# Group statistics by small DMA transfers instead of matrix products, a third output buffer, and a moved normalization, in a two-layer attention kernel

## The chip, the core and the metric

The kernel runs on one core of one Trainium2 chip. The metric is the device time of one execution in microseconds (us). The engines are called PE (TensorE, matrix products; PEld is its loading of weights), DVE (VectorE), ACT (ScalarE), POOL (GpSimd) and SP (SyncE, which only issues transfers). Each runs its own instructions in order and waits for others by semaphores. POOL and SP each have a queue of DMA transfers, in the order of their instructions.

## The reference

The input `x` is 4 images x 256 channels x 64 x 64, all in float32. Two layers are added to it, one after the other. Each first normalizes `x` over 32 groups of 8 channels, and it is this normalization that the change is about:

```python
def _gn(v, G=32, eps=1e-5):
    g = v.reshape(B_, G, C_ // G, H_, W_)
    m = jnp.mean(g, axis=(2, 3, 4), keepdims=True)
    s = jnp.var(g, axis=(2, 3, 4), keepdims=True)
    return ((g - m) / jnp.sqrt(s + eps)).reshape(v.shape)

x = x + _L0_conv_ref(_gn(x), ...)   # layer A below
x = x + _L1_conv_ref(_gn(x), ...)   # layer B below
```

Layer A is attention with 8 heads of 32 channels. Its queries are a 1x1 product of all 4096 points (`Wq`), its keys and values are 2x2 convolutions with stride 2 (1024 points), and a position term is added to the keys. Layer B takes q, k and v from one 1x1 product (`w_qkv`), attends within four areas of 1024 points, adds a 7x7 convolution of each channel's values, and ends in a 1x1 product (`w_proj`).

## The kernel before

**Units, steps, phases.** The attention of both layers is cut into 128 units: 8 blocks (layer A of images 0 to 3, then layer B of images 0 to 3) of 16 units, each unit being four heads and 512 queries. A unit has 8 steps, each of 128 keys. The main loop runs over 683 phases of one and a half steps. A phase issues, in this order: the scores of its own steps (PE, L428); the exponentials of them (ACT, L469 and L480); a slot of other work on PE; and the weighted sums of the phase before (PE, L494). DVE adds the exponentials up for the divisors (L504). The scores use three pairs of PSUM banks in turn, so the scores of a phase wait until ACT has emptied the pair that they write.

**The slot between.** In it stands one of four things: nothing; the divisors of a finished unit (`den`, L513); a function out of the list `quick`; or one, two or four "side parts". Side parts are the projections and convolutions, each cut with `yield` into two or four parts: q, k and v of layer A (`q0ps`, `k0ps`, `v0ps`), q and k of layer B (`q1ps`, `k1ps`), the values of layer B (`vals_ps`), the convolution (`conv_ps`, L1048) and the last product (`ops`). All but the convolution are issued by the helper at L167. How many parts a phase takes is set by the due times (`pressure`) and by `supply`, which spreads what is there and what will come over the next 24 phases at 13 slots in 16.

**The program is laid out by hand.** `at(g, j, f)` has `f` called at step `j` of unit `g`, and whatever `f` issues then goes to the ends of the engines' queues. What lies before unit 0 is issued ahead of the loop. `later(...)` puts normalizations (ACT, L392) into a list that is worked off when ACT has room, from a given phase on.

**Statistics.** `plan_norm` makes the scales of one normalization, called its key: A or B and the image. DVE aggregates the statistics of each channel (`aggregate`, L346); `means` multiplies them with `gmat`, a matrix of blocks of 1/8, so that each channel gets its group's mean (PE, L351), which ACT copies out of PSUM (L352); DVE adds each channel's squared deviation to its variance (L353 to L355); `variances` multiplies that with `gmat` again (PE, L359), ACT adds epsilon (L360), and POOL makes the reciprocal root and the shift (L363 to L368). In the loop, `means` and `variances` go through `soon` into `quick`, and a phase takes one of them if no task is begun, no unit ends in it, and the last was over two phases ago. A phase that takes one does no side part. Keys A of image 0 and A of image 1 are planned ahead of the loop, the other six inside it. The first reading of the scales is allowed four phases after they are `known`.

**Divisors.** For each finished unit, POOL issues `few` (L527), `recs` (L535) and four `rb` (L537) with DVE's reciprocals between them (L533), and DVE divides by `rb` (L540). The reciprocals are planned at step 0 of the second unit after, the division at step 7 of it.

**Values of layer B.** `values(t)` clears the edges of an output `vout` (DVE, L963 and L964), makes the product, copies it out (ACT, L975), and stores it twice (SP, L980 and L988: `vala` and `vals`). There are two buffers for `vout`. `load_v` loads a quarter of an area's values back from `vala` into one of four buffers `vc` (SP, L742), and `make_v` transposes it (DVE, L749). SP also loads the convolution's rows and matrices (`rows`, `share`, `band`, L1029 and L1032), in the same queue.

**q of layer A.** `fetch` loads a chunk `hq` (L108), and `norm_chunk` normalizes it from five phases after the load on.

Of the kernel before, what the change touches and what calls it, by code (L numbers as in the profile page):

```python
# [9 lines left out]
FP = mybir.dt.float32  # L10
# [5 lines left out]
P = 128  # L16
# [44 lines left out]
def direct_path(  # L61
# [129 lines left out]

    side, quick, quick_at = deque(), deque(), [-9]
    now, last = [-1], len(BLOCKS) * UNITS * NKT
# [20 lines left out]
    def supply():  # L214

        far = 24
        comes = [0] * (far + 1)
# [13 lines left out]
        for h in range(far):  # L231
            total += comes[h]
            least = min(least, total / max(1, (h + 1) * 13 / 16))
        return least
# [80 lines left out]

    def soon(f):

        if now[0] < 0:
            f()
        else:  # L320
            quick.append(f)

    stats, norms = {}, {}
# [11 lines left out]
    def plan_norm(key, g, j):  # L335

        name = f"{key[0]}{key[1]}"
        made = {}

        def aggregate():  # L340
            for tag, cols in (("mv", 2), ("gmean", 1), ("dev", 1), ("gvar", 1)):
                shape = [P, CT, cols] if cols > 1 else [P, CT]
                made[tag] = pool.tile(shape, FP, tag=tag, name=f"{tag}_{name}", bufs=2)
            mv = made["mv"]
            for t in range(CT):
                V.bn_aggr(out=mv[:, t, :], in_=stats[key][:, t].rearrange("p c s -> p (c s)"))  # L346
# [10 lines left out]
        def variances():  # L357
            ps = ps_side(f"gv_{name}")[:, :CT]
            T.matmul(ps, lhsT=gmat, rhs=made["dev"], start=True, stop=True)  # L359
            S.activation(made["gvar"], ps, AF.Identity, bias=eps)  # L360
            norm = pool.tile([P, 2, CT], FP, tag="norm", name=f"norm_{name}", bufs=8)
            shift, rstd = norm[:, 0, :], norm[:, 1, :]
            G.tensor_tensor(rstd, made["gvar"], neghalf, ALU.pow)  # L363
            if key == ("A", 0):
                V.scalar_tensor_tensor(shift, made["gmean"], -1.0, rstd, ALU.mult, ALU.mult)
            else:
                G.tensor_tensor(shift, made["gmean"], rstd, ALU.mult)
                G.tensor_scalar(shift, shift, -1.0, None, ALU.mult)  # L368
            norms[key] = shift, rstd
            known[key] = phase[0] if now[0] >= 0 else -4  # L370

        def quietly(f, n):
            f()
            if key == ("A", 0):
                keep_busy(n)

        if key == ("A", 0):
            at(g - 1, 0, lambda: keep_busy(44))
        at(g, j, aggregate)
        at(g, j + (2 if g >= 0 else 1), lambda: soon(lambda: quietly(means, 4)))  # L380
        at(g, j + (6 if g >= 0 else 3), lambda: soon(lambda: quietly(variances, 10)))

    def normalize(key, dst, src, t, by_vector=False):
        while key not in norms:
            while begun():
                advance()
            quick.popleft()()
        shift, rstd = norms[key]
# [162 lines left out]
    def plan_a(b, u, prep):  # L551
# [72 lines left out]
        for c in range(NCH):  # L624
            at(early + c // 2, 4 * (c % 2), lambda c=c: look(c))
            for t in range(CT):
                lag = (5 + 2 * t if b == 1 else 8 + 2 * t if b else 3)
                at(early + c // 2, 4 * (c % 2) + lag, lambda c=c, t=t: add_stats(c, t))
        plan_norm(key, early + (5 if b > 1 else 4), 3 if b > 1 else 4 if b else 1)
        for a in range(NAREA):  # L630
# [50 lines left out]
        for c in range(NCH):  # L681
            g = u + 2 * c
            at(g - 3, 4, lambda c=c: fetch(c))
            for t in range(CT):
                at(g - 2, 1 + 2 * t, lambda c=c, t=t: later(
                    ("hq", b, c), lambda: norm_chunk(c, t), after(key, fetched["q", c] + 5), True
                ))
# [17 lines left out]
    def plan_b(b, u):  # L705
# [34 lines left out]
        def load_v(a, n):  # L740
            vcs[a, n] = pool.tile([P, 2, 4 * TX, XT], FP, tag="vc", name=f"vc_{b}_{a}_{n}", bufs=4)
            nc.sync.dma_start(vcs[a, n], vala[b][a][:, :, 2 * n : 2 * n + 2].rearrange("t c h f x -> (t c) h f x"))  # L742
# [30 lines left out]
        for a in range(NAREA):  # L773
# [8 lines left out]
            for n in range(4):  # L782
                at(g - 4, 3 + 2 * n, lambda a=a, n=n: load_v(a, n))
                at(g - 2, 1 + 2 * n, lambda a=a, n=n: make_v(a, n))
        for c in range(NCH):
# [162 lines left out]
    def plan_values(b, c, start):  # L948
# [11 lines left out]
        def values(t):  # L960
            vout = pool.tile([P, RC, TX, XT], FP, tag="vout", name=f"vout_{b}_{c}_{t}", bufs=2)
            written.append(phase[0])
# [195 lines left out]
    before, credit = [], 0.0  # L1158
    while f < PHASES or before or plan or side or quick or norms_left or to_add or to_divide:
        now[0], phase[0] = step, f  # L1160
# [26 lines left out]
        elif due and not begun():  # L1187
# [6 lines left out]
            else:  # L1194
                rb = pool.tile([P, CH], FP, tag="p", name="rb", bufs=PB)
                V.reciprocal(rb, dens[g])
                spare.extend((dens.pop(g), rb))
        elif quick and not begun() and not cut and f < PHASES and f > quick_at[0] + 2:
            quick.popleft()()
            quick_at[0] = f  # L1200
        else:
# [14 lines left out]
        if f >= PHASES:  # L1216
            side_parts(2)
        if quick and f >= PHASES:
            quick.popleft()()
        while step < -(-3 * (f + 1) // 2):  # L1220
# [614 lines left out]
```

## Time and profile before

| | |
|---|---|
| median of 3 runs | 3063.1 us (3060.73 to 3066.85) |
| the profiled execution | 3063.53 us, its span 3061.5 us |
| mean granted clock of PE | 0.998 |
| exponential, 128x1024 (ACT, L469) | 1025 ns, x1194 |
| addition, 128x1024 (DVE, L504) | 1220 ns, x1790 |
| product with `gmat` (PE, L351 and L359) | 16 instructions each, 258 to 267 ns |
| `few`, `recs`, `rb` from issue to landing (POOL's queue) | 4.3, 3.8, 3.6 us in the median |
| HBM traffic over the span | 135 GB/s |

The page of the profile gives busy time by engine and, in 40 equal slices, the busy share in tenths, the granted clock of PE and the load of the 16 DMA engines. The timeline gives merged rows of one engine: start, duration, engine, line, what is written from what, how often, and in brackets the idle time before it and what ended that. Since products overlap in the array and their ends are modelled, the time that a block really took is the distance from its start to the next block's start. A list of waits has rows of "engine tile line <- what ended the wait: us in total, times, longest".

### The profile page before, as it was taken

How to read it: one execution, taken by the hardware profiler on the slowest of the kernel's cores; microseconds unless marked ns; L12 is line 12 of the kernel's file. 1: busy time of each engine (PE TensorE's matmuls, PEld its weight loads, DVE VectorE, ACT ScalarE, POOL GpSimd, SP SyncE). 2: the span in 40 equal slices, each digit the busy share in tenths (PEclk: the TensorE clock that was granted, in tenths of full speed). 3: DMA queues.
4: the chain of work that ended last, by engine and by line, in shares of the span. 5: the costliest groups of instructions: out<-in, count | busy, mean ns of one | idle time of the engine just before them, and what ended most of it. 6: DMA issues, size and time to landing. Idle time of an engine off the chain costs nothing.

```text
span 3061.5 us, 108320 instructions
## 1 busy us (share of the span) xinstructions
PE 3032.8 (99%) x47254; PEld 1280.0 (42%) x47254; DVE 2526.2 (83%) x2769; ACT 2455.9 (80%) x2988; POOL 433.8 (14%) x794
## 2 busy tenths in 40 slices
PE   9999999999999999999999999999999999999998
PEld 6444434444344444333444444444434444443332
DVE  3788988889887787878888888788878888888888
ACT  3888888888887888888888877788777787878885
POOL 0011111111111111111111111111111111111111
PEclk9999999999999999999999999999999999999999
DMA  5244533466354557777866677667755565553232
GB/s 191 51 101 98 126 92 73 109 142 165 83 140 133 143 152 175 189 161 194 204 175 162 156 176 185 152 171 178 176 127 145 144 159 143 149 139 79 50 71 62
DMA packets 644250, 422.73 MB, mean 138 GB/s; under 512 B 409740, under 2 KB 552572, under 8 KB 643768
## 3 DMA queue, kind: packets, MB, share of 16 engines
q1 hardware_dynamic: 619384, 380.11, 49.3%
q0 software_dynamic: 24384, 35.62, 5.1%
q8 instruction: 373, 6.11, 0.9%
q14 instruction: 109, 0.89, 0.1%
HBM read 317.28 MB, written 97.05 MB: 135 GB/s over the span
## 4 chain that ended last, share of the span: by engine, by line
PE 91%; DMA 3%; DVE 2%; ACT 2%; issue 2%; SPq 1%; POOL 0%; DVEq 0%; ACTq 0%; POOLq 0%
PE s L428 31%; PE av L494 26%; PE k0ps L167 4%; PE den L513 4%; PE v0ps L167 4%; PE q1ps L167 4%; PE k1ps L167 4%; PE conv_ps L1048 4%; PE q0ps L167 4%; PE ops L167 4%; PE vals_ps L167 3%; DVE acc L504 1%; ACT p L469 1%; DMA vals<-vout 1%; DMA rows<-vals 1%
## 5 line engine op out<-in xcount | busy, mean ns | idle before, releaser
L504 DVE TENSOR_TENSOR acc<-acc,p 128x1024 f32<-128x1024 f32 x1790 | 2117.4, 1220 | 382.7 <-PE av L494 285.7
L469 ACT ACTIVATE p<-s 128x1024 f32<-128x1024 f32 x1194 | 1159.8, 1025 | 419.3 <-PE s L428 407.6
L480 ACT ACTIVATE p<-s 128x1024 f32<-128x1024 f32 x598 | 619.8, 1036 | 1.5 <-DVE acc L504 0.7
L428 PE MATMUL s<-q,k_A 32*64 32x256 f32 (+1 forms) x10928 | 541.1, 494 | 4.1 <-ACT p L469 3.5
L428 PE MATMUL s<-q,k_B 32*64 32x512 f32 (+1 forms) x10912 | 537.1, 494 | 2.8 <-ACT p L469 2.4
L494 PE MATMUL av<-p,v_A 128*32 128x256 f32 (+1 forms) x4784 | 451.4, 486 | 0.0
L494 PE MATMUL av<-p,v_B 128*32 128x512 f32 (+1 forms) x4776 | 449.4, 487 | 0.0
L428 PEld LDWEIGHTS s<-q,k_B 32*64 32x64 f32 x10912 | 266.0, 130 | 325.1 <-PE s L428 60.4
L428 PEld LDWEIGHTS s<-q,k_A 32*64 32x64 f32 x10928 | 263.2, 130 | 329.1 <-PE s L428 58.5
L537 POOL DMA_DIRECT2D rb<-recs x508 | 251.4, 501 | 510.3 <-DMA recs<-few 497.9
L535 POOL DMA_DIRECT2D recs<-few x127 | 71.3, 561 | 1719.9 <-DVE sums L534 1600.3
L494 PEld LDWEIGHTS av<-p,v_B 128*32 128x32 f32 x4776 | 149.2, 110 | 264.5 <-issue 238.3
L494 PEld LDWEIGHTS av<-p,v_A 128*32 128x32 f32 x4784 | 149.5, 110 | 227.5 <-issue 186.0
L469 ACT ACTIVATE acc<-s 128x1024 f32<-128x1024 f32 x172 | 167.0, 1023 | 80.6 <-PE s L428 80.2
L513 PE MATMUL den<-acc,ones 128*32 128x512 f32 x1024 | 138.5, 605 | 0.9 <-DVE xm L831 0.9
L167 PE MATMUL ops<-cv,wp_sb 128*32 128x512 f32 x1024 | 126.6, 605 | 4.7 <-DVE xm L831 3.5
L527 POOL DMA_DIRECT2D few<-den_sb x127 | 90.5, 713 | 271.9 <-ACT den_sb L526 271.3
L167 PE MATMUL vals_ps<-hv,wqkv_sb 128*32 128x512 f32 x1024 | 124.9, 598 | 0.5 <-issue 0.5
L167 PE MATMUL q1ps<-h,wqkv_sb 128*32 128x512 f32 x1024 | 124.9, 599 | 0.0
L167 PE MATMUL k1ps<-h,wqkv_sb 128*32 128x512 f32 x1024 | 123.0, 597 | 1.7 <-ACT cout L1059 0.9
L167 PE MATMUL q0ps<-hq,wq_sb 128*32 128x512 f32 x1024 | 124.0, 597 | 0.1
L167 PE MATMUL k0ps<-taps,wkv 128*32 128x256 f32 x2048 | 123.9, 383 | 0.0
(102 smaller groups left out, 2089.5 us busy)
## 6 DMA issues: line engine op xcount, KB each, us to landing
rows<-vals SPq DMA_DIRECT2D x384, 195.9 KB
rb<-recs POOLq DMA_DIRECT2D x508, 64.0 KB, 3.6
share<-vals SPq DMA_DIRECT2D x128, 195.9 KB
vala<-vout SPq DMA_DIRECT2D x128, 144.0 KB
vals<-vout SPq DMA_DIRECT2D x128, 144.0 KB
vc<-vala SPq DMA_DIRECT2D x64, 288.0 KB
band<-mats SPq DMA_DIRECT2D x96, 176.0 KB
hq<-in_x SPq DMA_DIRECT2D x32, 512.0 KB
```

Of the source, the lines that this page charges most:

```text
L167: T.matmul(out[cols, :], lhsT=lhsT[:, cols], rhs=rhs, start=start, stop=stop)
L428: T.matmul(out[n : n + WIDE], lhsT=unit[2]()[rows, unit[0], j * P + n : j * P + n + WIDE], rhs=unit[1]()[rows, cols], start=True, stop=True,)
L469: S.activation(p, (a, b)[n], AF.Exp, scale=SCALE)
L480: S.activation(p, c.rearrange("p b (l n) -> p b l n", l=2), AF.Exp, scale=SCALE)
L494: T.matmul(out, lhsT=v[:, j, unit[0] * P + HD * h : unit[0] * P + HD * h + HD], rhs=rhs, start=(j == 0 and not u), stop=(j == NKT - 1), sk ...
L504: V.tensor_add(to, to, p)
L513: T.matmul(dens[g][HD * h : HD * h + HD, :], lhsT=ones, rhs=p(h), start=(n == 0), stop=(n == len(sets) - 1),)
L527: G.dma_start(few[:, 0, :], den_sb[0:P:HD, :].rearrange("h (q n) -> h q n", n=CH // HD))
L535: G.dma_start(recs.rearrange("h (q n) -> (h q) n", n=CH // HD), few[:, 1, :])
L537: G.dma_start(rb[HD * h : HD * h + HD, :], recs[h : h + 1, :].to_broadcast([HD, CH]))
L1048: T.matmul(ps[HD * m : HD * m + HD, (2 * k + i) * size : (2 * k + i + 1) * size].rearrange("p (y x) -> p y x", y=NY), lhsT=band[:, half].r ...
```

## The change

It has six parts.

1. For all keys but A of image 0, the group means and variances are no longer made by products. `gather` moves the channels' means and variances with two POOL transfers into 32 rows of 8 pairs, `of_groups` takes mean, variance of the means and sum of the variances along each row (DVE), and `scatter` makes the scale and shift (five POOL operations on 32 rows) and spreads them over the 128 channels with two POOL transfers. In the loop these are planned 1, 7 and 8 steps after `aggregate`; ahead of it 1, 2 and 3. A of image 0 keeps the products, without `quick`. The list `quick`, `soon` and the branch in the loop that served them are gone.
2. `supply` spreads over 14 slots in 16 instead of 13, and looks no further than the last phase.
3. The statistics of layer A of images 2 and 3 are added three steps later, and `aggregate` is one step later.
4. q of images 2 and 3 is normalized from seven phases after its load on, instead of five.
5. `vc` has three buffers instead of four; its loads are at steps 7, 9, 11 and 18 from the start of unit g-4, instead of 3, 5, 7 and 9; its transposes at 16, 18, 20 and 25, instead of 17, 19, 21 and 23.
6. `vout` has three buffers instead of two. The scales `norm` have four instead of eight.

```diff
-        far = 24
+        far = max(1, min(24, PHASES - phase[0]))
...
-            least = min(least, total / max(1, (h + 1) * 13 / 16))
+            least = min(least, total / max(1, (h + 1) * 14 / 16))
...
+        by_products = key == ("A", 0)
+        NG = P // 8
...
-            norm = pool.tile([P, 2, CT], FP, tag="norm", name=f"norm_{name}", bufs=8)
-            shift, rstd = norm[:, 0, :], norm[:, 1, :]
+            norm = pool.tile([P, CT, 2], FP, tag="norm", name=f"norm_{name}", bufs=4)
+            shift, rstd = norm[:, :, 0], norm[:, :, 1]
...
+        def gather():
+            by_group = made["by_group"] = pool.tile([CT * NG, 8, 2], FP, tag="by_group", name=f"by_group_{name}", bufs=1)
+            for t in range(CT):
+                G.dma_start(by_group[t * NG : (t + 1) * NG], made["mv"][:, t, :])
+
+        def of_groups():
+            by_group = made["by_group"]
+            for tag, cols in (("spread", 6), ("of_means", 2), ("within", 1), ("scale", 2)):
+                made[tag] = pool.tile([CT * NG, cols], FP, tag=f"group_{tag}", name=f"{tag}_{name}", bufs=1)
+            V.bn_stats(out=made["spread"], in_=by_group[:, :, 0])
+            V.bn_aggr(out=made["of_means"], in_=made["spread"])
+            V.tensor_reduce(made["within"], by_group[:, :, 1], AX.X, ALU.add)
+
+        def scatter():
+            scale, within, of_means = made["scale"], made["within"], made["of_means"]
+            shift, rstd = scale[:, 0:1], scale[:, 1:2]
+            G.tensor_scalar(within, within, 0.125, EPS, ALU.mult, ALU.add)
+            G.tensor_tensor(within, within, of_means[:, 1:2], ALU.add)
+            G.tensor_tensor(rstd, within, neghalf[: CT * NG, 0:1], ALU.pow)
+            G.tensor_tensor(shift, of_means[:, 0:1], rstd, ALU.mult)
+            G.tensor_scalar(shift, shift, -1.0, None, ALU.mult)
+            norm = pool.tile([P, CT, 2], FP, tag="norm", name=f"norm_{name}", bufs=4)
+            for t in range(CT):
+                G.dma_start(norm[:, t, :], scale[t * NG : (t + 1) * NG].unsqueeze(1).to_broadcast([NG, 8, 2]))
+            norms[key] = norm[:, :, 0], norm[:, :, 1]
             known[key] = phase[0] if now[0] >= 0 else -4
...
-        at(g, j + (2 if g >= 0 else 1), lambda: soon(lambda: quietly(means, 4)))
-        at(g, j + (6 if g >= 0 else 3), lambda: soon(lambda: quietly(variances, 10)))
+        at(g, j, aggregate)
+        if by_products:
...
+        else:
+            for n, f in (((1, gather), (7, of_groups), (8, scatter)) if g >= 0 else ((1, gather), (2, of_groups), (3, scatter))):
+                at(g, j + n, f)
...
-                lag = (5 + 2 * t if b == 1 else 8 + 2 * t if b else 3)
+                lag = (5 + 2 * t if b == 1 else 11 + 2 * t if b else 3)
...
-        plan_norm(key, early + (5 if b > 1 else 4), 3 if b > 1 else 4 if b else 1)
+        plan_norm(key, early + (5 if b > 1 else 4), 4 if b > 1 else 4 if b else 1)
...
-                    ("hq", b, c), lambda: norm_chunk(c, t), after(key, fetched["q", c] + 5), True
+                    ("hq", b, c), lambda: norm_chunk(c, t), after(key, fetched["q", c] + (7 if b > 1 else 5)), True
...
-            vcs[a, n] = pool.tile([P, 2, 4 * TX, XT], FP, tag="vc", name=f"vc_{b}_{a}_{n}", bufs=4)
+            vcs[a, n] = pool.tile([P, 2, 4 * TX, XT], FP, tag="vc", name=f"vc_{b}_{a}_{n}", bufs=3)
...
-                at(g - 4, 3 + 2 * n, lambda a=a, n=n: load_v(a, n))
-                at(g - 2, 1 + 2 * n, lambda a=a, n=n: make_v(a, n))
+                at(g - 4, 7 + 2 * n + 5 * (n == 3), lambda a=a, n=n: load_v(a, n))
+                at(g - 2, 0 + 2 * n + 3 * (n == 3), lambda a=a, n=n: make_v(a, n))
...
-            vout = pool.tile([P, RC, TX, XT], FP, tag="vout", name=f"vout_{b}_{c}_{t}", bufs=2)
+            vout = pool.tile([P, RC, TX, XT], FP, tag="vout", name=f"vout_{b}_{c}_{t}", bufs=3)
...
-        elif quick and not begun() and not cut and f < PHASES and f > quick_at[0] + 2:
-            quick.popleft()()
-            quick_at[0] = f
```

More of the change, by code (lines that the diff above doesn't have):

```diff
@@ L188, in at @@
         plan.setdefault((g, j), []).append(f)
-    side, quick, quick_at = deque(), deque(), [-9]
+    side = deque()
     now, last = [-1], len(BLOCKS) * UNITS * NKT
@@ L314, in normed @@
         return ready
[L316 to L321, printed above, removed]
     stats, norms = {}, {}
@@ L338, in plan_norm @@
         made = {}
+        by_products = key == ("A", 0)
+        NG = P // 8
         def aggregate():
[L341 to L344, printed above, removed]
+            mv = made["mv"] = pool.tile([P, CT, 2], FP, tag="mv", name=f"mv_{name}", bufs=2)
+            if by_products:
+                for tag in ("gmean", "dev", "gvar"):
+                    made[tag] = pool.tile([P, CT], FP, tag=tag, name=f"{tag}_{name}", bufs=1)
             for t in range(CT):
@@ L360, in variances @@
             S.activation(made["gvar"], ps, AF.Identity, bias=eps)
-            norm = pool.tile([P, 2, CT], FP, tag="norm", name=f"norm_{name}", bufs=8)
-            shift, rstd = norm[:, 0, :], norm[:, 1, :]
+            norm = pool.tile([P, CT, 2], FP, tag="norm", name=f"norm_{name}", bufs=4)
+            shift, rstd = norm[:, :, 0], norm[:, :, 1]
             G.tensor_tensor(rstd, made["gvar"], neghalf, ALU.pow)
[L364 to L368, printed above, removed]
@@ L369, in variances @@
-            norms[key] = shift, rstd
-            known[key] = phase[0] if now[0] >= 0 else -4
[L372 to L377, printed above, removed]
-            at(g - 1, 0, lambda: keep_busy(44))
-        at(g, j, aggregate)
-        at(g, j + (2 if g >= 0 else 1), lambda: soon(lambda: quietly(means, 4)))
-        at(g, j + (6 if g >= 0 else 3), lambda: soon(lambda: quietly(variances, 10)))
+            V.scalar_tensor_tensor(shift, made["gmean"], -1.0, rstd, ALU.mult, ALU.mult)
@@ new lines, in variances @@
+            norms[key] = shift, rstd
+            known[key] = -4
+        def gather():
[9 more added lines that the diff above has]
+            V.tensor_reduce(made["within"], by_group[:, :, 1], AX.X, ALU.add)
@@ L383, in normalize @@
+        at(g, j, aggregate)
+        if by_products:
+            at(g - 1, 0, lambda: keep_busy(44))
+            for n, f, more in ((1, means, 4), (3, variances, 10)):
+                at(g, j + n, f)
+                at(g, j + n, lambda more=more: keep_busy(more))
+        else:
+            for n, f in (((1, gather), (7, of_groups), (8, scatter)) if g >= 0 else ((1, gather), (2, of_groups), (3, scatter))):
+                at(g, j + n, f)
     def normalize(key, dst, src, t, by_vector=False):
-        while key not in norms:
-            while begun():
-                advance()
-            quick.popleft()()
@@ L1158, in direct_path @@
     before, credit = [], 0.0
-    while f < PHASES or before or plan or side or quick or norms_left or to_add or to_divide:
+    while f < PHASES or before or plan or side or norms_left or to_add or to_divide:
         now[0], phase[0] = step, f
@@ L1197, in direct_path @@
                 spare.extend((dens.pop(g), rb))
-        elif quick and not begun() and not cut and f < PHASES and f > quick_at[0] + 2:
-            quick.popleft()()
-            quick_at[0] = f
         else:
@@ L1217, in direct_path @@
             side_parts(2)
-        if quick and f >= PHASES:
-            quick.popleft()()
         while step < -(-3 * (f + 1) // 2):
```

## The prediction

> **What bounds the kernel now.** I read the busy shares first, then TensorE's timeline phase by phase, then the waits of VectorE and ScalarE that stand beside its losses.
>
> ```profile
> PE 3032.8 (99%) x47254; PEld 1280.0 (42%) x47254; DVE 2526.2 (83%) x2769; ACT 2455.9 (80%) x2988; POOL 433.8 (14%) x794
> ...
> PEclk9999999999999999999999999999999999999999
> ```
>
> TensorE is the bound, at nine tenths of its clock or more in every slice. But 99% hides its losses: a product that waits behind a full queue is drawn longer, not as idle time. They show in the distance from one block's start to the next:
>
> ```profile
> 1224.02 1.55 PE L428 MATMUL s<-q,k_A 32*64 32x256 f32 x32
> 1225.50 1.92 PE L167 MATMUL vals_ps<-hv,wqkv_sb 128*32 128x512 f32 x16
> 1227.24 1.47 PE L494 MATMUL av<-p,v_A 128*32 128x256 f32 x16
> 1228.64 1.55 PE L428 MATMUL s<-q,k_A 32*64 32x256 f32 x32
> ...
> 1231.81 2.00 PE L428 MATMUL s<-q,k_A 32*64 32x256 f32 x32 [0.20 <-ACT p L469]
> 1233.75 1.06 PE L513 MATMUL den<-acc,ones 128*32 128x512 f32 x8
> ...
> 1246.86 1.55 PE L428 MATMUL s<-q,k_A 32*64 32x256 f32 x32
> 1248.34 0.38 PE L351 MATMUL gm_B<-mv_B,gmat 128*128 128x2 f32 x2
> 1248.65 1.50 PE L494 MATMUL av<-p,v_A 128*32 128x512 f32 x16
> 1250.10 2.00 PE L428 MATMUL s<-q,k_A 32*64 32x256 f32 x32
> 1252.03 1.92 PE L167 MATMUL vals_ps<-hv,wqkv_sb 128*32 128x512 f32 x16
> ```
>
> The first phase has two side parts: scores 1.48, side 1.74, weighted sums 1.40, together 4.62 us, which is the pace of the products themselves. The next has no part: 3.17 us to the next scores, which then take 1.94 instead of 1.48, as they wait for ScalarE to empty their bank. So an empty phase costs 2.88 us of products and 0.29 + 0.46 = 0.75 us of loss. The phase of the group means (1246.86) costs 3.24 - 2.88 = 0.36, and 1.93 - 1.48 = 0.45 behind it. I walked all 683 phases so: with two parts or one, or with the divisors, they lose nothing as a rule; 30 are empty (22 us with what follows them), 12 hold a group product in the loop, and the loss of TensorE against its own pace is some 45 us in all. That is all this change can work on; the products themselves stay.
>
> One stretch loses for another reason:
>
> ```profile
> DVE vout L963 <- DMA vals<-vout: 6.5, 2, 4.7
> ACT vout L975 <- DMA vals<-vout: 3.9, 2, 2.4
> ...
> 1383.23 0.81 ACT L392 ACTIVATE hq<-hq,norm_A 128x512 f32<-128x512 f32 x1 [2.04 <-DMA hq<-in_x]
> ...
> 1388.28 0.70 ACT L975 ACTIVATE vout<-vals_ps,bqkv_sb 128x512 f32<-128x512 f32 x1 [1.50 <-DMA vals<-vout]
> ...
> 1388.33 0.07 DVE L963 MEMSET vout<- 128x16 f32 x1 [4.70 <-DMA vals<-vout]
> ```
>
> A values' output waits for the stores of the one two before it, and a normalization of q waits for its load, with both engines' queues behind them.
>
> **The sum, part by part**, against the profiled execution's own 3063.53 us (span 3061.5 and 2.0 around it; the median of the runs is 3063.1, 0.4 less, so both stand for each other).
>
> **Group products out.** Each costs 0.34 (3.22 of the usual phase, less 2.88) and about 0.43 behind it: 0.77 us. Seven keys lose two each. Six are normalized inside the loop, so 12 x 0.77 = 9.2 us, if their slots take side work. Work is there: after ten of the twelve a block of two or four parts follows at once, after the other two one follows the divisors. But side work is a fixed sum, and a part drawn forward is missing later; behind three of the six keys (phases 86 to 89, 282 to 300, 363 and 364) stand empty phases at 0.75 each. I count the other three keys' six slots whole and half of these: 9 x 0.77 = -6.9; bounds 0 and -9.2. The key of image 1's first layer is done at the loop's start, where the scores wait for q's copy anyway: only one pair of 0.31 is gained, -0.3.
>
> **Small transfers in.** Per key, GpSimd gets two gathers, five operations on 32 rows and two scatters in place of three operations. The nearest rows are its DMA issues `few<-den_sb` (0.71 us) and its operations on two columns (0.2 to 1.6 us): some 3 us of issue and 3 us of work, against about 3 us before, on an engine busy 14%. What is queued behind it are the divisors' transfers `recs` and `rb`, which VectorE's division waits for; these come at step 0 of a unit, the scatter at step 3 or 4, 9 us or more later, and the division only at step 7. VectorE's statistics of groups wait for the gather: 2 issues and one landing (4.3 us median of `few<-den_sb`, 8.3 at most) make 6 to 10 us, and six steps of 2.96 us give 17.8. The scatter takes about 5 us of operations and issue and the same landing, and its readers start four phases, 18 us, later. So zero is taken; if the cover failed, six keys x (10 - 2.4) us (2.4: see below) would be lost at worst, +46, or nothing gained below zero: ScalarE's and VectorE's freed 1 us is not on TensorE's path.
>
> The Trainium skill speaks against this edit (DMA: Bandwidth & Descriptors, "Rules for kernel authors": many small transfers should be made one large one, since below 64 KB most of the time is overhead; "Anatomy of one DMA" gives about 2 us fixed each). This trace's 8 KB transfers take 3.8 to 4.3 us to land, twice that. By the page the two in series would add an estimated 4 us to a key's statistics, by the rows 8; either lies in the 17.8 and 18 us of cover, and the sum stays the same.
>
> **When the statistics are known.** Plan against plan: image 2's scales come out in phase 78, where the second product ran in phase 81; the others come one or two phases earlier. Behind it stand phases 86, 87 and 89, empty because the taps could be normalized only four phases after (losses with what follows, 2.2 us). Three phases earlier fills about half: -1.0; bounds 0 and -2.2.
>
> **Third output buffer, and q two phases later.** The losses of phases 271 (1.37), 303 (1.24, the q wait), 304 (1.64) and 305 (0.63) are 4.9 us. With a third buffer the two late outputs wait for the stores before, issued by 1214.1 and 1362.3, an estimated 8.1 us (their median landing) ahead of being free: 1222 and 1370, long before 1239 and 1383. The load of q has two phases, 8 us, more where it lacked 2.04. All of it is taken, -4.9; bounds -2 (another queue's wait takes their place) and -4.9. Moving q's normalization leaves 6 of the 13 phases between fetch and use; the statistics' three steps more for images 2 and 3 take away waits of 3.3 us in all on VectorE, the longest 3.04, behind which TensorE lost 0.16. Both at 0; if q came late, 16 chunks x 0.75 = +12 at worst.
>
> **Values' loads: one buffer less and later.** The loads of `vc` are issued four steps later and the transposes one step earlier; the last load nine steps later, its transpose two: 14 steps between them become 9 (-14.8 us) and for the last 7 (-20.7). In the trace the last load of the 16 areas stands 19.2 to 51.9 us ahead of its transpose, as SyncE's queue runs late. These are the tightest:
>
> ```profile
> 1598.94 0.35 SPq L742 DMA_DIRECT2D vc<-vala  x1
> ...
> 2080.36 0.47 SPq L742 DMA_DIRECT2D vc<-vala  x1
> ```
>
> Their transposes start at 1625.29 and 2100.03. Landing took 5.4 us in the median and 9.3 at most (by the semaphore's steps after each issue). So 26.0 - 20.7 = 5.3 against that area's 7.1: a wait of 1.8; 19.2 - 20.7 = -1.5 against 3.6: 5.1; the other areas none. A wait of 1.8 us on VectorE (1368.45) cost TensorE nothing, one of 4.70 (1388.33) cost 1.64 + 0.63: VectorE forgives 2.4 us. So +2.7; with 9.3 us for each landing, seven areas wait 23 us and TensorE pays 10.8. Bounds 0 and +10.8.
>
> **Supply rule.** The reserve is spread over 14/16 instead of 13/16 slots, 7% thinner: fewer double phases early, more parts left. The trace doesn't show which wins. Eight of the 30 empty phases either way, 8 x 0.75: bounds -6 and +6, taken 0, as the work is a fixed sum. The horizon cut at the end raises the rate of the last 24 phases, where nine are empty and six parts are left behind the loop; these cost VectorE 1.4 us in the closing chain. Bounds -1.4 and +0.8, taken 0.
>
> Sum: -6.9 - 0.3 - 1.0 - 4.9 + 2.7 = -10.4; 3063.5 - 10.4 = **3053.1 us**. Its own range is 3046 to 3058.
>
> **Rivals.**
> (1) *The freed slots only go empty.* For it: an empty phase costs 0.75, a quick one 0.77; the same work remains. Against it: two-part blocks right behind ten of the twelve. Then -10.4 + 6.9 = -3.5: 3060. Chance 17%.
> (2) *Slower: the last value load stalls VectorE in every area.* With three buffers that load waits at the head of SyncE's queue for the first transpose, and everything behind it goes late. The gains are 13.1 us, so it decides once the 16 areas pay 0.8 each, a mean wait of 3.2 us. At 4 us: 16 x 1.6 = 25.6, and 3063.5 - 13.1 + 25.6 = 3076. For it: slacks of 5 us and less in two areas, and SyncE's lateness; against it: 27 us and more between load and transpose in 14 areas, 39 to 52 in four of them. Chance 16%.
> (3) *The thinner supply also fills the empty phases*: 3053.1 - 6 - 1.4 = 3046. For it: 414 double phases stand beside 30 empty ones; against: many are empty because nothing is ready. Chance 10%.
> The forecast has 57%.
>
> **The numbers.** 0.2% of the time, 6.1 us, is what a measurement can tell from no change. Faster: most of 57%, all of 10%, a little of (1), 65%. Same: most of (1) and the forecast's upper edge, 17%. Slower: (2) and a remainder, 18%. The range reaches from 3042, under (3), to 3067, over (1) and the foot of (2).
>
> **What would show it.** L351 and L359 left with two matmuls each; no wait of `vout` on `vals<-vout`, nor of `hq` on its load; phases 86 to 90 with parts; the number of empty phases near 30. Wrong it would be by waits of VectorE at L749's transposes, by ScalarE waiting for `norm`, or by more than 40 empty phases.

## The result, and the profile after

The changed kernel is slower: 3084.35 us in the median of four runs (3081.48 to 3086.56), against 3061.91 (3059.12 to 3066.85) for the kernel before on the same chip. The estimated ratio is 1.0063, with a 95% interval of 1.0051 to 1.0075. The profiled execution took 3082.59 us, its span 3080.9, so 19.1 more than the 3063.53 of before; the forecast was 10.4 less.

From line 392 on, the lines of before stand 13 lower in the changed kernel (the scores L428 are L441, the weighted sums L494 are L507, the values' output L975 is L988).

Most of what the prediction looked for did happen. This is TensorE's timeline of the changed kernel at phase 272 (the prediction counts phases from 1), where before had `gm_B`:

```profile
1256.36 1.55 PE L441 MATMUL s<-q,k_A 32*64 32x256 f32 x32
1257.83 1.92 PE L167 MATMUL vals_ps<-hv,wqkv_sb 128*32 128x512 f32 x16
```

The slot carries two side parts. Over the loop there are 31 empty phases against 30, none with a group product, and 106 with one part against 90. Of phases 86 to 90, which should have had parts, 87 and 89 are still empty, and one wait of `hq` for its load is left, of 1.5 us. The waits of `vout` for its stores, 6.5 us on VectorE and 3.9 on ScalarE before, are gone. In their place stand these, of which before has none (VectorE's and ScalarE's waits for transfers, in total, times, longest):

```profile
DVE xc L686 <- DMA xc<-in_x: 15.7, 4, 6.8
...
DVE v_B L762 <- DMA vc<-vala: 2.6, 3, 1.3
...
ACT hv L405 <- DMA hv<-xmid: 13.2, 2, 11.4
```

Loads of chunks come late, which the prediction had not looked at; the loads of `vc`, which it had feared, hardly do. The page of the whole shows little of it: a hundredth less of TensorE's share, a busy share of 8 tenths instead of 9 in the tenth of the 40 slices (693 to 770 us), and 7 instead of 8 in the last:

```profile
PE 3030.9 (98%) x47226; PEld 1291.6 (42%) x47226; DVE 2525.5 (82%) x2769; ACT 2454.8 (80%) x2974; POOL 467.0 (15%) x836
...
PE   9999999998999999999999999999999999999997
```

So I followed the start of each phase's scores in both kernels. The table gives how much later (+) or earlier (-) than in the profile of before a phase begins, in us. Here phases count from 0, so 682 is the last. The other rows are experiments, told of below. Runs before on the chips of the experiments had medians of 3058.5 to 3064.3, so some 5 us of a difference between a profile and the profile of before can be the chip's. Jumps within a row are not touched by that.

| phase | 128 | 144 | 160 | 304 | 328 | 681 | end |
|---|---|---|---|---|---|---|---|
| after (all parts) | -5.8 | -1.5 | +14.3 | +11.1 | +15.9 | +12.6 | +19.4 |
| e3 (part 1) | -6.7 | -6.7 | -5.1 | -7.1 | -8.8 | -10.8 | -8.4 |
| e6 (parts 1, 5, 6) | -7.3 | -7.3 | -5.9 | -14.3 | -16.0 | -18.7 | -17.1 |
| e1 (all but part 3) | -7.6 | -7.6 | -0.1 | -1.0 | +3.6 | +0.3 | +6.6 |
| e4 (seven chunk buffers) | -7.5 | -7.5 | -4.3 | -7.5 | -3.3 | +1.1 | +7.0 |
| e2 (before, with part 3) | -3.8 | -3.8 | +3.5 | +1.2 | +1.2 | +3.3 | +3.1 |
| e7 (before, with part 4) | -1.9 | -1.9 | -2.3 | +5.2 | +18.3 | +15.0 | +14.2 |

The change leads by 5.8 us at phase 128, loses 20.1 up to phase 160, and 6.8 from phase 681 to the end. Busy time by stretch of the changed kernel and then of the kernel before, for 700 to 750 us (columns: stretch, its length, busy us of PE, PEld, DVE, ACT, POOL, PE's granted clock, DMA share, GB/s):

```profile
700.00:750.00 50.00, 40.65 (x564) 14.89 (x560) 33.49 (x43) 31.35 (x38) 4.46 (x9) 0.90 0.69 169
```

```profile
700.00:750.00 50.00, 50.00 (x755) 19.89 (x744) 43.74 (x58) 42.03 (x52) 7.19 (x13) 1.00 0.71 173
```

Every engine does less, TensorE stands for 9.4 us, and its granted clock falls to 0.90. What it waits for begins 40 us earlier, in SyncE's queue (its timeline in the changed kernel):

```profile
667.76 0.38 SPq L108 DMA_DIRECT2D hq<-in_x  x1
684.82 0.37 SPq L108 DMA_DIRECT2D xs<-in_x  x1
...
708.17 0.47 SPq L968 DMA_DIRECT2D hv<-xmid  x1
```

Before, the same two loads (`hv` is L955 there) are issued 7 and 13 us earlier:

```profile
677.68 0.37 SPq L108 DMA_DIRECT2D xs<-in_x  x1
...
695.43 0.33 SPq L955 DMA_DIRECT2D hv<-xmid  x1
```

In the changed kernel nothing is issued between 668.1 and 684.8. The load of `xs`, a chunk for the statistics, needs one of the six buffers named `chunk`, which `xs`, `xa`, `hq`, `hv`, `xc` and others share (L104). SyncE's waits from 560 to 730 us name what held it, `add_stats`; the first fence is the changed kernel, the second before:

```profile
SPq L108 <- DVE st_A L577: 29.6, 2, 16.6
```

```profile
SPq L108 <- DVE st_A L564: 18.9, 3, 6.8
```

SyncE works in order, so the load of `hv` behind it comes at 708.17, and ScalarE stands for it (ScalarE's timeline), and TensorE for ScalarE (TensorE's):

```profile
711.70 0.81 ACT L405 ACTIVATE hv<-hv,norm_B 128x512 f32<-128x512 f32 x1 [11.39 <-DMA hv<-xmid]
```

```profile
714.39 2.90 PE L441 MATMUL s<-q,k_A 32*64 32x256 f32 x32 [9.28 <-ACT p L482]
717.22 3.41 PE L167 MATMUL vals_ps<-hv,wqkv_sb 128*32 128x512 f32 x16
720.46 1.46 PE L507 MATMUL av<-p,v_A 128*32 128x256 f32 x16
```

The reader is to see two losses: the idle 9.28 us, and the two blocks after it, which take 2.83 and 3.24 from start to start where 1.48 and 1.74 are usual. That second loss is 2.85 us.

### The profile page after: what moved, and what is told of

Same layout as the page of the kernel before. It is cut to its first block, busy times and chain, and to the rows that moved or that the text cites. A ratio compares the mean times of both kernels' runs of the same rounds, so it can differ in the third digit from the quotient of the medians.

```text
span 3080.9 us, 108322 instructions
## 1 busy us (share of the span) xinstructions
PE 3030.9 (98%) x47226; PEld 1291.6 (42%) x47226; DVE 2525.5 (82%) x2769; ACT 2454.8 (80%) x2974; POOL 467.0 (15%) x836
## 4 chain that ended last, share of the span: by engine, by line
PE 90%; DVE 3%; DMA 2%; ACT 2%; issue 2%; SPq 1%; POOL 0%; DVEq 0%; ACTq 0%; POOLq 0%
PE s L441 31%; PE av L507 26%; PE q1ps L167 4%; PE conv_ps L1061 4%; PE v0ps L167 4%; PE k0ps L167 4%; PE den L526 4%; PE k1ps L167 4%; PE q0ps L167 4%; PE vals_ps L167 3%; PE ops L167 3%; DVE acc L517 2%; ACT p L482 1%; DMA rows<-vals 1%; ACT p L493 0%
## 5 line engine op out<-in xcount | busy, mean ns | idle before, releaser
L441 PE MATMUL s<-q,k_A 32*64 32x512 f32 (+1 forms) x10928 | 542.8, 496 | 16.0 <-ACT p L482 14.6
L441 PE MATMUL s<-q,k_B 32*64 32x512 f32 (+1 forms) x10912 | 534.7, 494 | 2.8 <-ACT p L482 2.6
L507 PE MATMUL av<-p,v_A 128*32 128x256 f32 (+1 forms) x4784 | 451.2, 486 | 1.2 <-issue 1.2
L507 PE MATMUL av<-p,v_B 128*32 128x512 f32 (+1 forms) x4776 | 449.9, 487 | 0.0
L441 PEld LDWEIGHTS s<-q,k_A 32*64 32x64 f32 x10928 | 264.5, 130 | 344.9 <-ACT p L482 70.5
L441 PEld LDWEIGHTS s<-q,k_B 32*64 32x64 f32 x10912 | 267.1, 130 | 323.0 <-PE s L441 61.6
L507 PEld LDWEIGHTS av<-p,v_B 128*32 128x32 f32 x4776 | 149.3, 110 | 265.4 <-issue 239.8
L507 PEld LDWEIGHTS av<-p,v_A 128*32 128x32 f32 x4784 | 150.4, 110 | 233.3 <-issue 190.9
```

Of the source, the lines that this page charges most:

```text
L441: T.matmul(out[n : n + WIDE], lhsT=unit[2]()[rows, unit[0], j * P + n : j * P + n + WIDE], rhs=unit[1]()[rows, cols], start=True, stop=True,)
L507: T.matmul(out, lhsT=v[:, j, unit[0] * P + HD * h : unit[0] * P + HD * h + HD], rhs=rhs, start=(j == 0 and not u), stop=(j == NKT - 1), sk ...
```

## The experiments

All times are medians beside the kernel before on the same chip. Part numbers are those of the change; the four buffers of `norm`, named under part 6, go with part 1 here.

| kernel | parts | median us | before | difference | ratio, 95% interval |
|---|---|---|---|---|---|
| e3_before_transfers | 1 | 3055.21 | 3058.50 | -3.3 | 0.9988 [0.9978, 0.9997] |
| e6_transfers_buffers | 1, 5, 6 | 3048.26 | 3059.44 | -11.2 | 0.9962 [0.9948, 0.9976] |
| e5_stats_early_q5 | 1, 2, 5, 6 | 3063.75 | 3059.44 | +4.3 | 1.0012 [1.0003, 1.0022] |
| e1_stats_early | 1, 2, 4, 5, 6 | 3066.41 | 3058.50 | +7.9 | 1.0023 [1.0013, 1.0032] |
| after | 1 to 6 | 3084.35 | 3061.91 | +22.4 | 1.0063 [1.0051, 1.0075] |
| e11_before_buffers | 5, 6 | 3055.78 | 3058.99 | -3.2 | 0.9992 [0.9982, 1.0001] |
| e2_before_stats_late | 3 | 3065.67 | 3058.50 | +7.2 | 1.0019 [1.0010, 1.0029] |
| e7_before_q7 | 4 | 3078.86 | 3059.44 | +19.4 | 1.0062 [1.0045, 1.0078] |
| e8_transfers_supply | 1, 2 | 3072.26 | 3059.44 | +12.8 | 1.0046 [1.0029, 1.0063] |
| e9_supply_14 | 1, 5, 6, 14/16 | 3058.62 | 3058.99 | -0.4 | 0.9997 [0.9987, 1.0007] |
| e10_horizon_cut | 1, 5, 6, cut | 3052.84 | 3058.99 | -6.2 | 0.9980 [0.9971, 0.9990] |

Read as a chain, the first five rows give each step by differences of the differences: part 1 -3.3, parts 5 and 6 -7.9, part 2 +15.5, part 4 +3.6, part 3 +14.5. By the intervals a row is known to 3 or 4 us and a step to 4 or 5, so the +3.6 of part 4 is not clear of zero.

**Part 3 undone and alone.** My first theory was that the later statistics alone carried the loss.

```diff
-                lag = (5 + 2 * t if b == 1 else 11 + 2 * t if b else 3)
+                lag = (5 + 2 * t if b == 1 else 8 + 2 * t if b else 3)
...
-        plan_norm(key, early + (5 if b > 1 else 4), 4 if b > 1 else 4 if b else 1)
+        plan_norm(key, early + (5 if b > 1 else 4), 3 if b > 1 else 4 if b else 1)
```

(e1; e2 is the reverse of it, made to the kernel before)

> The changed kernel with its part 3 alone undone (statistics of layer A of images 2 and 3 again 8 steps after the load instead of 11, aggregate again one step earlier). Theory H (buffers held): the later statistics keep each loaded chunk three steps, 8.9 us, longer in the six buffers that xs, xa, hq, hv, xc and others share, so SyncE's queue stands still at a load (16.6 us before 684.8) and everything behind it comes late; then TensorE's loss of 17.8 us between 650 and 750 us falls under 3, and the time comes to 3066 (3062 to 3070). Rival T (transfers: the new GpSimd transfers or the emptied slots do it): 3080 and more, with the stalls near 655 and 705 still there. Rival Q (q two phases later does it): the stalls stay too.

> The kernel before with part 3 alone done (statistics 11 steps after the load, aggregate one step later). Theory H: the load of a chunk waits on SyncE for a buffer by 10 us or more between 640 and 720 us, ACT waits for hv or xa there, and the time is 3075 to 3083. Rivals T and Q: no such wait, 3060 to 3064.

Undone, it gives back 14.5 us (22.4 - 7.9); alone it costs 7.2, less than I had expected. The place is right: e2 goes from -3.8 to +3.5 between phases 144 and 160, where the change loses 15.8. But the theory was too small: with part 3 undone the kernel is still slower than before, and e1 still loses 7.5 there, where I had expected under 3.

**Part 1 alone, and with the buffers.**

> The kernel before with part 1 alone done (statistics by transfers, the list quick gone); parts 2 to 6 are as before. Theory H with the forecast's own term: 12 slots are freed at 0.77 us each, 9 of them worth it, so 3055 (3052 to 3059). Rival 1 of the prediction (freed slots only go empty): 3061 to 3062, with about 42 empty phases instead of 30. Rival T: 3070 and more.

> The changed kernel with parts 2, 3 and 4 undone: transfers and the buffers of vout and vc alone. The closing stretch behind the last scores is 4 us shorter than with the new supply rule (30 us instead of 34, as with the transfers alone), the loop the same: 3 to 5 us under the run with parts 1, 2, 5 and 6; against the transfers alone -3 to -5 if the third output buffer gives its 4.9 us, 0 if another wait takes their place.

> The kernel before with parts 5 and 6 alone (third buffer of vout, three buffers of vc at their new places). By the prediction -4.9 us for the waits of vout, and up to +2.7 for the loads of vc: -2 to -5 against the kernel before. Between the transfers alone and the transfers with these buffers lay 7.9 us, which would make it -8. Rival 2 of the prediction (VectorE stalls at the last value load of every area): slower than the kernel before, with waits of 3 us and more at L749.

Part 1 is a gain. Parts 5 and 6 alone come out 3.2 us faster, with an interval that reaches 1.0001. In e6, VectorE's longest wait for a residual chunk is 0.7 us and no wait for `vc` or `vout` is left. e6 has the lowest ratio of all and beats both kernels. The two together (-11.2) come out above the sum of the two alone (-3.3 - 3.2), but by no more than the intervals leave open.

**Parts 2 and 4.** Like part 3, these two had been taken as worth nothing.

> The changed kernel with parts 3 and 4 undone (statistics and normalization of q at their old places). Theory H extended: q normalized two phases later also holds a chunk buffer 8 us longer, and with the third output buffer the wait has moved to the residual's load xc, which comes late for want of a buffer. Then the 7.5 us that the kernel with part 3 undone still lost between phases 144 and 160 and its waits of 10.9 us on xc go, and the time is 7 to 11 us under that kernel: from +7 over the kernel before to between 0 and -4. Rival S (the supply rule or the third output buffer itself crowds the queue): within 2 us of the kernel with part 3 undone, xc's waits still there.

> The kernel before with parts 1 and 2 (transfers and the supply rule). If the supply rule costs the closing stretch: the same loop as with transfers alone within 2 us, and 3 to 5 us more behind the last scores, in all about the time of the kernel before. If the rule is neutral, as forecast: the time of the transfers alone, 3 to 4 us under the kernel before.

> The kernel before with part 4 alone (q of images 2 and 3 normalized from seven phases after the load on). Theory H extended: +4 to +8 us over the kernel before, with loads waiting on SyncE for a buffer after 690 us and xc or hv late. Rival: the forecast's zero, or -1.2 for the one wait of hq on its load: -2 to +1.

```diff
-                    ("hq", b, c), lambda: norm_chunk(c, t), after(key, fetched["q", c] + 5), True
+                    ("hq", b, c), lambda: norm_chunk(c, t), after(key, fetched["q", c] + (7 if b > 1 else 5)), True
```

(e7, on the kernel before)

I had e5 no slower than before, e6 3 to 5 us under e5, e8 at about the time of before, and e7 at a few us over it. They came out at +4.3, 15.5 under e5, +12.8 and +19.4. Part 2 costs 15.5 us (e5 against e6) or 16.1 (e8 against e3). Part 4 costs 19.4 where `vout` has two buffers.

SyncE's waits in e7 show the held chunk. Between 600 and 800 us a chunk's load waits 31.5 us for q's product, where before waits 18.7 at most. That one cost TensorE nothing: e7's row of the table stays at -1.9 to -2.3 from phase 128 to 160. Between 1200 and 1460 us the load of `hv` (L955) waits for q's product:

```profile
SPq L955 <- PE q0ps L167: 5.5, 1, 5.5
```

It is issued at 1274.38, and the stores of `vout` that stand behind it in the queue only at 1283.40. SyncE's, ScalarE's and TensorE's timelines:

```profile
1283.40 1.12 SPq L980 DMA_DIRECT2D vala<-vout  x2
```

```profile
1294.96 0.70 ACT L975 ACTIVATE vout<-vals_ps,bqkv_sb 128x512 f32<-128x512 f32 x1 [4.72 <-DMA vals<-vout]
```

```profile
1295.72 3.65 PE L1048 MATMUL conv_ps<-rows,band 88*32 88x128 f32 x64 [3.35 <-ACT vout L975]
```

VectorE's and ScalarE's waits over the span grow from the 6.5 and 3.9 of before:

```profile
DVE vout L963 <- DMA vals<-vout: 15.2, 3, 8.0
...
ACT vout L975 <- DMA vals<-vout: 15.0, 3, 7.6
```

A chunk of q that is used two phases later gives its buffer back later; the load behind it stands, then the stores of `vout` behind that, and then the next output. The largest loss of e7, a wait of 6.37 us of TensorE for an output at 1421.28, also follows stores of `vout`, but in the 80 us ahead of it no load waits over 2.0 us for a chunk's buffer; how part 4 leads there isn't shown. With the third `vout` buffer part 4 costs 3.6 (e1 against e5). That the missing link makes the difference is argued: e5 also has parts 1, 2 and 5.

Part 4 also makes q late for its reader. In the four kernels that have it (the changed one, e1, e4, e7), and in no other, three phases issue q's product in the midst of the scores that read it. TensorE in the changed kernel:

```profile
1282.45 0.66 PE L441 MATMUL s<-q,k_A 32*64 32x256 f32 x8
1283.04 1.92 PE L167 MATMUL q0ps<-hq,wq_sb 128*32 128x512 f32 x16
1284.89 1.52 PE L441 MATMUL s<-q,k_A 32*64 32x512 f32 x24
```

The next phase starts at 1289.49, 7.04 us after this one. At the pace of its products it would take 1.48 + 2 x 1.74 + 1.40 = 6.36, so 0.68 is lost in each of the three, some 2 us in all.

**A seventh chunk buffer.** If held buffers are the cause, the changed plan must be cheap with one more of them. Room for it was taken from `vout` and `vc`.

```diff
-        return pool.tile([P, CT, CH], FP, tag="chunk", name=name, bufs=6)
+        return pool.tile([P, CT, CH], FP, tag="chunk", name=name, bufs=7)
...
-            vcs[a, n] = pool.tile([P, 2, 4 * TX, XT], FP, tag="vc", name=f"vc_{b}_{a}_{n}", bufs=3)
+            vcs[a, n] = pool.tile([P, 2, 4 * TX, XT], FP, tag="vc", name=f"vc_{b}_{a}_{n}", bufs=2)
...
-            vout = pool.tile([P, RC, TX, XT], FP, tag="vout", name=f"vout_{b}_{c}_{t}", bufs=3)
+            vout = pool.tile([P, RC, TX, XT], FP, tag="vout", name=f"vout_{b}_{c}_{t}", bufs=2)
```

> The changed kernel, all its plans kept, with seven chunk buffers instead of six; to make room vout has two buffers and vc two. Theory H: with a seventh buffer the late statistics hold nothing up, TensorE's loss between 650 and 750 us falls from 17.8 to under 4. Rivals T and Q: it stays over 12. The whole time isn't told by this, as two buffers of vc may cost up to 15 us behind 1500 us.

Part 3 is kept, and between phases 144 and 160 e4 loses 3.2 us instead of 15.8. The stretch and SyncE's waits from 560 to 730 us, as above:

```profile
700.00:750.00 50.00, 49.82 (x748) 19.48 (x744) 44.11 (x56) 41.47 (x50) 7.55 (x14) 1.00 0.64 158
```

```profile
SPq L108 <- DVE st_A L577: 14.7, 3, 6.4
```

The wait of 16.6 is gone with the plan unchanged: for this stretch the buffers are shown as the cause. Over all, e4 takes 3072.41 (+13.9). It still has part 2, and two buffers of `vc` now make VectorE wait 19.4 us, five times, and two of `vout` 13.1 us; how the 13.9 divides among these isn't shown. e15, told of below, has e4's buffers without parts 3 and 4 and the cut, and takes +11.9. So with seven buffers these three cost 2.0 us together (known to some 6), where with six buffers parts 3 and 4 cost 18.1, without the cut.

**The supply rule, taken apart.** e9 adds 14/16 to e6, e10 the cut at the last phase.

```diff
-            least = min(least, total / max(1, (h + 1) * 13 / 16))
+            least = min(least, total / max(1, (h + 1) * 14 / 16))
```

(e9)

```diff
-        far = 24
+        far = max(1, min(24, PHASES - phase[0]))
```

(e10)

> Transfers and the buffers of vout and vc (the fastest kernel so far, 11.2 us under the kernel before), with 14 slots in 16 instead of 13 in the supply rule, the horizon uncut. Theory H for the supply: fewer parts per phase leave q and values made later, so the chunks they read are held longer, and loads stand still; the loop gets 10 to 14 us longer between phases 128 and 304, and the kernel ends 8 to 14 us over the fastest. Rival C (the cut horizon does it): within 2 us of the fastest.

> The same fastest kernel with the horizon cut at the last phase, 13 slots in 16. The cut acts in the last 24 phases only. If the longer closing stretch (34 us instead of 30 behind the last scores) is the cut's: +3 to +5 us, the loop up to phase 656 unchanged. If it is the thinner supply's: within 1 us of the fastest.

14/16 costs 10.8 us (-0.4 + 11.2) and the cut 5.0 (-6.2 + 11.2), together 15.8, near the 15.5 of part 2. The cut is clear. e10 has 29 empty phases against 32 in e6, as intended, but from phase 681 to the end it takes 4.6 us more. From the last scores on, the kernels with part 1 and with q's loads on SyncE take 29.6 to 30.4 us without the cut (e3, e6, e9, e14, e15) and 32.6 to 34.4 with it (e1, e4, e5, e8, e10, after). TensorE's and VectorE's timelines there, for e6 and then for e10:

```profile
3024.86 3.64 PE L167 MATMUL ops<-cv,wp_sb 128*32 128x512 f32 x32 [2.14 <-DVE xm L844]
```

```profile
3024.07 0.74 DVE L844 SCALAR_TENSOR_TENSOR xm<-ops,bproj_sb,xm 128x512 f32<-128x512 f32 x1
...
3025.72 3.33 DVE L1209 RECIPROCAL rb<-den 128x512 f32<-128x512 f32 x1
```

```profile
3032.42 4.92 PE L167 MATMUL ops<-cv,wp_sb 128*32 128x512 f32 x32 [4.67 <-DVE xm L844]
```

```profile
3027.52 3.35 DVE L1209 RECIPROCAL rb<-den 128x512 f32<-128x512 f32 x1
...
3031.65 0.72 DVE L844 SCALAR_TENSOR_TENSOR xm<-ops,bproj_sb,xm 128x512 f32<-128x512 f32 x1
```

With other parts left over, VectorE's last reciprocal, 3.35 us, comes ahead of the addition that frees TensorE's bank. TensorE waits 4.67 instead of 2.14 and then runs slower. The changed kernel ends in the same order (a wait of 5.02, then 5.62 for the same product).

For 14/16 I had two theories. In e9 SyncE waits at chunk loads for q's products 56.5 us, against 18.7 in e6, and at stores of `vout` for ScalarE 34.8, against 14.9 (e6 first):

```profile
SPq L108 <- PE q0ps L167: 18.7, 4, 7.0
```

```profile
SPq L108 <- PE q0ps L167: 56.5, 7, 26.0
```

Both grow, which fits projections that come later. One stall follows, of ScalarE in e9 (its timeline) and then, for 5.85 us at 1384.16, of TensorE:

```profile
1381.48 0.81 ACT L405 ACTIVATE hq<-hq,norm_A 128x512 f32<-128x512 f32 x1 [6.71 <-DMA hq<-in_x]
```

To tell the held chunk from the queue itself, I took e4's buffers with 13/16 (e14: parts 1 and 5, two `vout`, two `vc`, seven chunk buffers) and with 14/16 (e15); and, on six buffers, e6 (e17) and e9 (e16) with q's loads on GpSimd's queue:

```diff
-        nc.sync.dma_start(xc, xv[b][:, :, c * CH : (c + 1) * CH])
+        queue = G if name == "hq" else nc.sync
+        queue.dma_start(xc, xv[b][:, :, c * CH : (c + 1) * CH])
```

> The small transfers and the later value loads, with seven chunk buffers, two vout and two vc buffers; supply rule, statistics and q as before. It is the base of the next kernel. Both theories: 3050 to 3060 us, the missing third vout buffer and the thin vc buffers costing some 5 us over the transfers with three of each (3048.26).

> The kernel of e14_seven with the supply rule's 14/16 and nothing else. With six chunk buffers 14/16 cost 13.7 us in the profiles (e9 against e6). Theory that the sparser supply costs because projections come later and hold chunk buffers longer: the seventh buffer takes it up, and this kernel is at most 4 us over e14_seven. Rival, that SyncE's queue stands at the stores of projections that come late, which a chunk buffer does not mend, or that the sparser supply costs by itself: 8 to 14 us over e14_seven.

> The transfers, the buffers and 14/16 (the kernel of e9), with the loads of q's chunks (hq) given to GpSimd's queue instead of SyncE's. The seventh chunk buffer did not take up the cost of 14/16 (10.1 us in the profiles of e15 and e14). Theory: the cost is that the load of hq stands in SyncE's queue behind stores of projections that are made later; on another queue it is early, ScalarE's wait of 6.7 us at about 1377 goes, and this kernel is at most 5 us over its own base e17. Rival: the sparser supply costs by itself, or GpSimd's queue stands as long: 9 to 14 us over e17.

> The transfers and the buffers (the kernel of e6, 3048.26), with the loads of q's chunks given to GpSimd's queue: the base of e16, differing from it in 14/16 alone. Both theories: 3045 to 3052 us, as no load of hq was waited for in e6.

| kernel | median us | before | ratio, 95% interval |
|---|---|---|---|
| e14_seven | 3064.04 | 3059.51 | 1.0018 [1.0009, 1.0028] |
| e15_seven_14 | 3071.42 | 3059.51 | 1.0035 [1.0022, 1.0047] |
| e17_q_gpsimd | 3055.32 | 3064.30 | 0.9975 [0.9965, 0.9984] |
| e16_q_gpsimd_14 | 3066.18 | 3064.30 | 1.0009 [0.9999, 1.0018] |

The two bases came out above what I had expected, e14 at 3064 for 3050 to 3060 and e17 at 3055 for 3045 to 3052. e15 is 7.4 us over e14 (10.0 in the profiles). That lies between the two ranges set for it, at most 4 and 8 to 14: as the whole explanation, the held chunk is unlikely, and ScalarE still waits for `hq`, 7.8 us at 1384. e16 is 10.9 over e17, so the queue theory falls, in its simple form. In e16's profile ScalarE's wait for `hq` is gone, but that execution, 3058.65 us, was the fastest of ten, and shows no more than 1.4 us over e17 at phase 681; what the others lost can't be read from it.

The starts of the phases show two places. Between phases 144 and 160 the kernels with part 1 and 13/16 lose 1.4 to 1.5 us (e3, e6, e14, e17), those with 14/16 and six chunk buffers 4.8 to 6.0 (e5, e8, e9, e16), and e15, with seven, 2.7: there a seventh buffer takes up 2.5 us of e9's 3.8 over e6. Between phases 160 and 304 e9 loses 10.0 us against e6, and with seven buffers e15 still loses 8.6 against e14. That 14/16 costs 7 to 11 us is shown three times over; by which way it costs most of it is open.

**GpSimd's end.** In every kernel with the small transfers GpSimd closed later. e13 is the kernel before with four further transfers of `mv` for each normalization but A of image 0, into a tile that nothing reads; the four buffers of `norm` make the room for it.

```diff
+            if key != ("A", 0):
+                spare_rows = pool.tile([CT * 16, 8, 2], FP, tag="by_group", name=f"by_group_{name}", bufs=1)
+                for n in range(2):
+                    for t in range(CT):
+                        G.dma_start(spare_rows[t * 16 : (t + 1) * 16], mv[:, t, :])
...
-            norm = pool.tile([P, 2, CT], FP, tag="norm", name=f"norm_{name}", bufs=8)
+            norm = pool.tile([P, 2, CT], FP, tag="norm", name=f"norm_{name}", bufs=4)
```

> The kernel before, its products kept, with four further small transfers on GpSimd's queue for each normalization (rows of mv into a tile that nothing reads) and four buffers of norm instead of eight. It adds as many GpSimd transfers as the change does and none of its 32-row operations. If the longer closing drain of GpSimd (1.70 us before, 4.40 us in every kernel with the small transfers) comes from the number of transfers on its queue, the drain here is near 4.4 us. If it comes from the 32-row operations or the broadcasting transfers, it stays at 1.70 us. The time itself should stay within 4 us of the kernel before under both.

One run took 3062.45 us, beside 3059.51. The drain is 4.40 us without any operation on 32 rows: it follows the transfers.

## Why the prediction was wrong

**Step by step.** *Group products out* and *small transfers in* at 0: right in kind. Part 1 gives -3.3 in the median where the terms for it, with *statistics known earlier*, were -8.2. GpSimd's end, for which the sum had no term, gives 2.3 us of it back (last section), so some -5.6 in the loop; e3's profile has -10.8 there, with the chip's difference in it. *Statistics known earlier*, -1.0, no run measures alone; two of the three phases that it was to help fill are still empty. The rule that spoke against the edit, in the Trainium skill's page "DMA: Bandwidth & Descriptors", "Rules for kernel authors" (make one large transfer of many small ones), did not decide: the trace has no wait of ScalarE for the scales from these transfers, and VectorE's one wait for a gather, 3.7 us, lies ahead of the loop.

*Third output buffer*, -4.9, and *values' loads*, +2.7 (sum -2.2): the first mechanism was right and stands in the traces, as `vout`'s waits are gone. The second was mis-sized: VectorE waits for `vc` 2.6 us in the changed kernel and not at all in e6, so it is near 0. Parts 5 and 6 gave -3.2 alone (an interval that reaches zero) and -7.9 on top of part 1.

*"Both at 0"*, of moving q's normalization and the later statistics: this step failed. The prediction asked whether what was moved would be late for its reader. For the statistics it was not; q was, in three phases, at some 2 us in all, within the +12 that the prediction allowed as its worst. It did not ask how long the moved reader holds its input. Part 3 cost 14.5 us on top of the others (7.2 alone); 12.6 of it lies between phases 128 and 160 (20.1 in the changed kernel, 7.5 in e1), where the seventh buffer shows held buffers as the cause. Part 4 cost 3.6, not clear of zero (19.4 alone), by q's lateness and, as far as e7's trace goes, by held buffers. The lower bound for the third buffer, where "another queue's wait takes their place", was the right thought on the wrong part. So was rival 2: a load stood at the head of SyncE's queue for a buffer and all behind it went late, but at the chunks and not at `vc`.

*Supply rule*, "taken 0, as the work is a fixed sum", bounds -6 and +6, and the cut, bounds -1.4 and +0.8: this failed too, at +10.8 and +5.0, both outside their bounds. The sum of products is fixed, and the empty phases moved by three, from 32 to 29 in e9 and in e10, not by eight. But the rule moves every projection, with SyncE's and VectorE's order around it. For the cut that is shown in the closing chain; for 14/16 the cost is shown, and held chunks for some 2.5 us of it (phases 144 to 160).

*Rival 1* (the freed slots go empty) is refuted by 31 empty phases and none with a group product. *Rival 3* (the thinner supply fills the empty phases) is refuted by e9: three empty phases fewer, and 10.8 us more.

By the chain of medians the 22.4 us are -3.3 - 7.9 for what was costed, and +15.5 + 3.6 + 14.5 for what was put at nothing.

## What to carry to other kernels

When a use is moved later, cost the buffer that it holds as well as the deadline that it meets: find the next load that takes the same buffer, and all that stands behind that load in its in-order queue. A load that stands is not yet a loss (31.5 us in e7 cost nothing); it becomes one when something behind it is late for its reader. A share of 98 or 99% busy hides such stalls; the start of each phase, compared between two traces, shows where they begin. Where a change bundles gains with retimings, try the gains without them: here parts 1, 5 and 6 alone make the kernel 0.4% faster than before, and the rest turned that into 0.6% slower.

## What the runs showed of the hardware

**GpSimd's end grows with its transfers.** From GpSimd's last instructions in each trace (its semaphore update `INC_SWDGE_SEM` and the `DRAIN` behind it), with transfers added to the 762 of before:

| kernel | added | INC_SWDGE_SEM us | DRAIN us |
|---|---|---|---|
| before | 0 | 0.61 | 1.70 |
| e13, e3, e6, after | 28 | 1.27 | 4.40 |
| e17 | 60 | 2.46 | 9.30 |

The two together grow by 3.4 us in the changed kernel and by 9.45 in e17. They lie behind all computing. Before, GpSimd's drain ends at 3059.64 and SyncE's own closing at 3060.67, so the first 1.0 us of the growth is covered: from the last scores on, e13 takes 2.0 us more than before, e3 2.3 and e17 8.6. It isn't in proportion to the transfers in all, and 32 of e17's 60 are loads of whole chunks; what it goes by is open.

**A wait of TensorE can cost more than its length.** The same 32 products (`ops`, near the end) took 3.64 us after a wait of 2.14 (e6), but 5.34 after 2.10 (e9), 5.31 after 3.05 (before), 4.92 after 4.67 (e10) and 5.62 after 5.02 (after); scores took 2.90 instead of 1.55 after 5.85 and after 9.28. The granted clock is 1.00 throughout e6's 3.64 us, and 0.50 from 3039.0 to 3042.0 us in e9. The Trainium skill has this in "TensorE: Matmul & The Clock Gate", Part 1: half the clock after an idle window of about 3.4 us. The runs agree on the half, but not on a wait of that length: 2.10 was enough once, and 2.14 was not.
